# A two-layer graph network: the own half normalised in a later stage, counts and ranks from summed one-hots, and a new order of the sorting stage

## The chip, the cores and the metric

The kernel runs on one core of a Trainium2 chip. TensorE (PE) multiplies matrices and loads its weights (PEld), VectorE (DVE), ScalarE (ACT) and GpSimd (POOL) work elementwise, and SyncE (SP) issues most transfers. The metric is the device time of one execution in microseconds, the median of several. Lower is better.

## The reference

There are 12500 nodes with 256 features and 200000 edges `src`, `dst`, sorted by `dst`. The first layer, cut to what matters (4 heads of 32):

```python
feat = relu(einsum('nd,ohdk->ohnk', feat_in, W) + b)        # o = 0: own half, o = 1: neighbour half
att_s = leaky(feat[0] . a_self); att_n = leaky(feat[1] . a_neigh)
edge_w = (att_s[:, row] + att_n[:, col]) * adj_vals          # row = src, col = dst
agg = segment_sum(edge_w * feat[1][:, col], row)
feat = stack([feat[0], agg])
feat = (feat - mean) * scale * rsqrt(var + 1e-9) + offset    # per head, both halves
x = layernorm(x + concat(own half, aggregated half))
```

The second layer:

```python
messages = relu(concat(x[src], x[dst]) @ W_msg + b_msg)
h = relu(concat(x, segment_sum(messages, dst)) @ W_upd + b_upd)
x = layernorm(x + layernorm(h) * gamma + beta)
```

## The kernel before

The work runs in three stages, one after the other.

**Sorting stage.** The edges are sorted by `dst` but the first layer sums by `src`, so this stage writes every message into a log in DRAM, placed by the block of 128 source nodes that it belongs to (98 blocks). It goes over 112 groups of 14 tiles of 128 edges. `sort_tasks(g)` makes, for a group, the one-hots `A` of the blocks of its edges (`widen`, `hot`, `hot_b`: partition = edge, 14 tiles x 99 blocks, the first seven tiles in one instruction and the last seven in another). `ranks` counts the edges of each block with 14 matmuls of a 99-column one-hot with a column of ones. `quarter` and `rows` make log rows of the counts. `begins` adds, for each block, 14 matmuls of a triangular matrix with the one-hots. `place_mm0` to `place_mm2` and 14 `pick` instructions on ACT turn that into a slot for each edge, and `split`, `hot_r`, `hot_q`, `goods` and `permute` bring the edges' data into slot order. What is then needed as a row instead of a column, the destination of each slot, goes through DRAM and back: `rel_keep`, `rel_turn`, `rel_row`, `rel_out` (to `reld`), `rel_in` (back into `rr`, 512 KB, broadcast over the partitions), `hot_n` (one-hots `oT` of the destinations). Six `message` steps multiply these with the neighbour features (`F3`), six `evict` steps on ACT copy the result into the tile `m` (three buffers, of which `extras` on DVE writes two columns), and four `scatter` steps on POOL write `m` into the log.

Beside it, `feat_tasks(g)` computes the features: a window of destination nodes for the neighbour half, for all groups, and block `g` of nodes for the own half, for the first 98 groups. `transposes`, `keep`, `project`, `relu`, the attention sums and `centre` work on both halves at once. For the own half the stage also does the whole head normalisation and writes the first layer's partial result, `y` = x + offset + the normalised own half, to `yd` (`offsets`, `square`, `var`, `root`, `rstd`, `norm`, `scale`, `put`, `out_y`). `meta_tasks` prepares, once for eight groups, the edges' indices and weights (lines 325 to 406).

PE, ACT, DVE and SP run their instructions in the order in which the program gives them, written out by hand: the table `AT` gives each step a time in units of which a group has 256 (`TG`), all steps of all groups are sorted by `256 * g + AT[step]`, and each engine gets its instructions in this order. A step may stand several groups later than its group's first one. POOL's order is left to the framework.

**Middle stage.** It sums the log, block by block: five pieces to a block, loaded up to nine pieces ahead into twelve buffers (`log_load`), multiplied with attention on POOL (the fifth piece on DVE) and turned into one-hots on DVE (`log_hot`), and summed on PE two steps later (`log_sum`). Batches of up to four blocks then have their aggregated half normalised (`heads_a` to `heads_d`, the last on POOL), are added to `y`, which `load_y` fetches from `yd` with one load into three buffers, get the layernorm's sums, are multiplied with the message weights and stored (`proj_*`, `store_x1`). This order too is by steps: `work[t]` holds what is issued at step `t`, five steps to a block.

**Edge stage.** It gathers the projected source rows by edge, adds the destination part, applies relu, sums by destination and finishes the nodes.

Of the kernel before, what the change touches and what calls it, by code (L numbers as in the profile page):

```python
# [11 lines left out]
def _warn_once_fixed(msg, *args, **kwargs):  # L12
# [6 lines left out]
FT = mybir.dt.float32  # L19
FR = mybir.dt.float32r  # L20
BF = mybir.dt.bfloat16
I32 = mybir.dt.int32
AF = mybir.ActivationFunctionType
OP = mybir.AluOpType
AX = mybir.AxisListType

P = 128
D = 256
HD = 128
H = 4  # L30
GT = 14
# [6 lines left out]


AT = {  # L40
    "widen": -140, "hot": -47, "hot_b": 3, "ranks": 44, "quarter": 71, "rows": 78, "begins": 155,
    "keep_begins": 189, "keep_v": 180, "shift": 218, "reach": 377, "steps": 314, "steps_keep": 337,
    "steps_low": 358, "target": 474, "index": 554, "place_mm0": 207, "place_mm1": 281, "place_mm2": 370,
    "pick0": 224, "pick1": 255, "pick2": 256, "pick3": 299, "pick4": 305, "pick5": 305, "pick6": 312,
    "pick7": 368, "pick8": 401, "pick9": 408, "pick10": 435, "pick11": 456, "pick12": 457, "pick13": 481,
    "split": 523, "hot_r": 547, "goods": 577, "hot_q": 563, "permute": 636, "rel_keep": 663, "extras": 717,
    "rel_turn": 685, "rel_row": 708, "rel_out": 738, "rel_in": 884, "hot_n": 885, "message0": 965,
    "evict0": 985, "message1": 1004, "evict1": 1046, "message2": 1006, "evict2": 1074, "message3": 1051,
    "evict3": 1132, "message4": 1092, "evict4": 1150, "message5": 1140, "evict5": 1200, "scatter0": 1078,
    "scatter1": 1124, "scatter2": 1163, "scatter3": 1210, "load": -363, "transposes": 234, "keep": 250,  # L50
    "project": 290, "relu": 308, "offsets": 441, "att_mult": 334, "mean_sum": 371, "att_sum": 404,
    "centre": 388, "leaky_n": 494, "part0": 507, "part1": 678, "part2": 741, "part3": 780, "leaky_s": 899,
    "square": 476, "var": 595, "root": 656, "rstd": 792, "norm": 814, "scale": 916, "put": 941, "out_y": 1139,
    "m_load": -1372, "m_cast0": -982, "m_cast1": -1209, "m_col0": -970, "m_keep0": -940, "m_col1": -414,
    "m_keep1": -359, "m_col2": -655, "m_keep2": -607, "m_block": -852, "m_place": -776, "m_high": -348,
    "m_rest": -26, "m_mid": 2, "m_low": 358, "m_win": -179, "m_turn": -654, "m_pairs": -648, "m_mask": -313,
    "m_count": 101,
}
BIG = 4096.0
MAGIC = 1.5 * 2.0 ** 23  # L60
# [1 line left out]
BB = 4  # L62
# [40 lines left out]
def kernel(  # L103
# [19 lines left out]
    nc = tc.nc  # L123
    N = x.shape[0]
# [5 lines left out]
    ROWS = NB * P  # L130
# [10 lines left out]
    dram = ctx.enter_context(tc.tile_pool(name="dram", bufs=1, space=bass.MemoryType.DRAM))  # L141
    NBX = NB + 1
# [3 lines left out]
    reld = dram.tile([NG, P * NR], BF, name="reld")  # L146
    x1d = dram.tile([ROWS, D], FT, name="x1d")
    pd = dram.tile([ROWS, D], FT, name="pd")
    yd = dram.tile([ROWS, D], FT, name="yd")

    def bcast_row(ap1d, n):
        return ap1d.rearrange("(o n) -> o n", o=1).to_broadcast([P, n])
# [17 lines left out]
    epsh = consts.tile([P, 1], FT, name="epsh")  # L170
# [23 lines left out]
    scb = consts.tile([P, D], FT, name="scb")  # L194
    ofb = consts.tile([P, D], FT, name="ofb")
# [22 lines left out]
    with ExitStack() as l0:  # L218
# [3 lines left out]
        feat = l0.enter_context(tc.tile_pool(name="feat", bufs=2))  # L222
        srt = l0.enter_context(tc.tile_pool(name="srt", bufs=2))
# [14 lines left out]
        lessb = dcp.tile([P, P], BF, name="lessb")  # L238
        onesb = dcp.tile([P, 1], BF, name="onesb")
# [174 lines left out]
        xb = {}  # L414
        F3 = {}
# [13 lines left out]
        def feat_tasks(g):  # L429
# [4 lines left out]
            st = {}  # L434
# [20 lines left out]
                nc.scalar.copy(xT[:, a:z].rearrange("p c q -> p (c q)"), st["tp"][:, a * P:z * P])  # L455
                st["xT"] = xT

            def offsets():
                st["y"] = feat.tile([P, D], FT, name="y", bufs=3)
                nc.vector.tensor_tensor(st["y"], xb[g], ofb, op=OP.add)  # L460

            def project():
                fp = bank[g][:, 0:D] if ww else ps.tile([P, 512], FT, name="fs")[:, 0:D]
                nc.tensor.matmul(fp[:, lo:hi], ones3, bias3[:, lo:hi], start=True, stop=False)
# [52 lines left out]
                a = st["a"][:, 0:H]  # L517
                nc.vector.scalar_tensor_tensor(atts[:, g, :], a, 0.2, a, op0=OP.mult, op1=OP.max)

            def square():  # L520
                st["q"] = feat.tile([P, HD], FT, name="q")
                nc.scalar.activation(st["q"], st["F"][:, 0:HD], AF.Square)

            def var():
                st["v"] = feat.tile([P, H], FT, name="v")
                nc.vector.tensor_reduce(st["v"], st["q"].rearrange("p (h k) -> p h k", h=H), AX.X, OP.add)

            def root():
                nc.scalar.activation(st["v"], st["v"], AF.Sqrt, bias=epsh, scale=1.0 / 32)

            def rstd():
                nc.vector.reciprocal(st["v"], st["v"])

            def norm():
                c = st["F"][:, 0:HD].rearrange("p (h k) -> p h k", h=H)
                nc.vector.tensor_tensor(c, c, st["v"][:, :, None].to_broadcast([P, H, 32]), op=OP.mult)

            def scale():
                c = st["F"][:, 0:HD]
                nc.vector.tensor_tensor(c, c, scb[:, 0:HD], op=OP.mult)  # L540

            def put():
                nc.vector.tensor_tensor(st["y"][:, 0:HD], st["y"][:, 0:HD], st["F"][:, 0:HD], op=OP.add)

            def out_y():
                nc.sync.dma_start(yd[g * P:(g + 1) * P, :], st["y"])

            w = lambda f: f if ww else None
            k = lambda f: f if bb else None
            return dict(transposes=transposes, keep=keep, project=project, relu=relu, offsets=k(offsets),  # L550
                        att_mult=att_mult, mean_sum=mean_sum, att_sum=att_sum, centre=centre, leaky_n=w(leaky_n),
                        part0=w(part(0)), part1=w(part(1)), part2=w(part(2)), part3=w(part(3)),
                        leaky_s=k(leaky_s), square=k(square), var=k(var), root=k(root), rstd=k(rstd),
                        norm=k(norm), scale=k(scale), put=k(put), out_y=k(out_y))

        scatters, zeros = [], []
        zero = dcp.tile([P, RW * MW], FT, name="zero")
# [10 lines left out]
        def sort_tasks(g):  # L568


            c, j = divmod(g, GC)
            tl = slice(j * GT, (j + 1) * GT)
            st = {}
# [6 lines left out]
            h = GT // 2  # L580
# [9 lines left out]
            def hot_b():  # L590
                b = blk[c][:, j * GT + h:j * GT + GT, None].to_broadcast([P, h, NBX])
                nc.vector.tensor_tensor(st["A"][:, h:], iotab[:, h:], b, op=OP.is_equal)  # L592
                st["C"] = [st["A"][:, i] for i in range(GT)]

            def ranks():
                bank[g] = ps.tile([P, 512], FT, name="fs")
                st["sm"] = bank[g][:, D + P:]
                st["V"] = bank[g][:, D:D + NBE]
                for i, v in enumerate(st["C"]):
                    nc.tensor.matmul(st["sm"][:NBX, 0:1], v, onesb, start=(i == 0), stop=(i == GT - 1))  # L600

            def quarter():
                nc.scalar.activation(small("rows"), st["sm"][:NBX, 0:1], AF.Identity, bias=quart[:NBX], scale=1.0 / RW)
# [5 lines left out]
            def begins():  # L609
                r = st["rows"]  # L610
                nc.tensor.matmul(st["sm"][:NBX, 1:2], less[:NBX, :NBX], r, start=True, stop=True)
                nc.tensor.matmul(st["V"], r.to_broadcast([NBX, P]), less4[:NBX, :NBE],
                                 start=True, stop=False)
                for i, v in enumerate(st["C"]):
                    nc.tensor.matmul(st["V"][:, :NBX], lessb, v, start=False, stop=(i == GT - 1))

            def keep_begins():
                st["b0"] = begun[:, g:g + 1]
# [126 lines left out]
            def scatter(k):  # L745
                def f():
# [7 lines left out]
                    for p in zeros[-16:] if g >= GZ else zeros[:nz0] if g < 2 else []:  # L754
                        tc.add_manual_dep(ins, p.name, sync_dep, reason="the rows left over are zero")
                return f

            tasks = dict(widen=widen, hot=hot, hot_b=hot_b, ranks=ranks, quarter=quarter,
                         rows=rows, begins=begins, keep_begins=keep_begins, keep_v=keep_v, shift=shift, reach=reach,
                         steps=steps, steps_keep=steps_keep, steps_low=steps_low, target=target, index=index)  # L760
            tasks.update((f"place_mm{i}", place_mm(i)) for i in range(3))
# [2 lines left out]
                         extras=extras, rel_turn=rel_turn, rel_row=rel_row, rel_out=rel_out, rel_in=rel_in, hot_n=hot_n)  # L764
# [33 lines left out]
        work = defaultdict(list)  # L798
# [113 lines left out]
    with ExitStack() as bar:  # L912
        lgp = bar.enter_context(tc.tile_pool(name="lgp", bufs=12))
        bw = bar.enter_context(tc.tile_pool(name="bw", bufs=2))
# [17 lines left out]
        NK = len(PART)  # L932
# [132 lines left out]
            nc.scalar.activation(t, ys[q][:, i], AF.Identity, bias=nmr[:, b:b + 1], scale=rsd[:, b:b + 1])  # L1065
            nc.sync.dma_start(x1d[b * P:(b + 1) * P, :], t)

        ys = {}

        def load_y(q):  # L1070
            b, n = spans[q]
            ys[q] = bw.tile([P, BB, D], FT, name="y", bufs=3)
            nc.sync.dma_start(ys[q][:, :n], yd[b * P:(b + n) * P, :].rearrange("(b p) w -> p b w", p=P))

        def centre_proj():

# [18 lines left out]
        for q, (b, n) in enumerate(spans):  # L1095
            t0 = (b + n) * NK + 3
            for d, f in ((0, heads_a), (1, heads_s), (2, heads_b), (3, heads_r), (4, heads_c), (5, heads_d),
                         (8, stats), (9, root), (10, rstd), (10, offset)):
                work[t0 + d].append(lambda q=q, f=f: f(q))
            work[b * NK].append(lambda q=q: load_y(q))  # L1100
            for i in range(n):
                for d, f in ((8, proj_t), (9, proj_k), (11, proj_m), (13, proj_s), (13, store_x1)):
                    work[t0 + d + (NK - 1) * i].append(lambda b=b, i=i, f=f: f(b + i))
            tend = max(tend, t0 + 13 + (NK - 1) * (n - 1))
# [512 lines left out]
```

## Time and profile before

| | |
|---|---|
| median of 3 runs | 4087.51 us (4082.6 to 4089.36) |
| profiled execution | 4089.95 us, span 4088.2 us |
| granted TensorE clock, mean | 0.989 |
| busy over the span | PE 88%, DVE 78%, POOL 62%, ACT 60% |
| first sum of the middle stage | 1155.4 us |
| last sum of the middle stage | 2062.1 us |

The profile page gives busy times by engine, the span in slices, the chain of waits that ended last and the costliest groups of instructions. A group is named by its line, engine and operation, with the tile written, an arrow and the tiles read. The shares over the whole span mix three stages with different limits, so what a change is worth has to be read from the busy times and waits of its own stage.

### The profile page before, as it was taken

To read this page: it belongs to the slowest core of one execution; us is meant where nothing else is said; L and a number is where in the kernel's file an instruction comes from. 1 tells how busy PE (TensorE), PEld (TensorE's weight loads), DVE (VectorE), ACT (ScalarE), POOL (GpSimd) and SP (SyncE) were. 2 spreads that over 40 slices of the span, in tenths; PEclk is the share of its full clock that TensorE was granted. 3 is DMA by queue.
4 is the path that set the end of the run, shared out by engine and by line. 5 is a ranking of instruction groups with operands and counts; after the bars stand their busy time and mean duration, and the time that the engine had idled before them with its cause. 6 is when DMAs were issued, how large, how long until landed. Compare 5 with 4: busy or idle time off the path is not lost.

```text
span 4088.2 us, 86328 instructions
## 1 busy us (share of the span) xinstructions
PE 3580.6 (88%) x26432; PEld 3016.1 (74%) x26432; DVE 3197.3 (78%) x9815; ACT 2465.8 (60%) x8632; POOL 2549.4 (62%) x2461
## 2 busy tenths in 40 slices
PE   7999999999989999999978878787888787787776
PEld 6888888887878888888866666666666666666665
DVE  8999999999878888888856666667666666666666
ACT  7999999999922222222246555555565555555555
POOL 2555555554455555555557777777777777777775
PEclk9999999999999999999999999999999999999999
DMA  5777766665566666666656666666666666666664
GB/s 183 261 259 260 258 221 209 208 209 192 195 204 183 186 185 180 184 186 185 182 148 169 171 171 171 169 171 171 171 170 172 169 173 168 169 173 169 169 171 129
DMA packets 457248, 763.85 MB, mean 187 GB/s; under 512 B 75772, under 2 KB 300574, under 8 KB 456782
## 3 DMA queue, kind: packets, MB, share of 16 engines
q1 hardware_dynamic: 326622, 415.17, 35.7%
q0 software_dynamic: 110848, 327.87, 26.2%
q10 hardware_dynamic: 19312, 15.21, 1.2%
q8 instruction: 216, 3.54, 0.4%
q14 instruction: 250, 2.05, 0.2%
HBM read 553.43 MB, written 204.54 MB: 185 GB/s over the span
## 4 chain that ended last, share of the span: by engine, by line
PE 34%; DMA 24%; DVE 23%; ACT 8%; issue 5%; POOL 4%; DVEq 0%; ACTq 0%; POOLq 0%; SPq 0%
DMA gb<-pd,srcf 21%; PE sum L966 20%; PE agg L1364 6%; DVE gb L1345 4%; POOL gb L1286 4%; ACT gb L1347 3%; DVE mv L685 2%; PE qp L1323 2%; PE qm L1054 2%; ACT junk L667 2%; DVE qh L690 2%; DMA rr<-reld 1%; DVE oT L725 1%; DVE A L592 1%; DMA reld<-rT 1%
## 5 line engine op out<-in xcount | busy, mean ns | idle before, releaser
L1286 POOL DMA_INDIRECT gb<-pd,srcf x1563 | 1510.2, 966 | 511.5 <-issue 266.8
L1364 PE MATMUL agg<-gb,o 128*128 128x256 f32 x3126 | 860.6, 398 | 271.5 <-ACT gb L1347 268.4
L1345 DVE TENSOR_TENSOR gb<-qp,gb 128x512 f32<-128x512 f32 x781 | 538.5, 690 | 653.6 <-DMA gb<-pd,srcf 501.0
L1347 ACT ACTIVATE gb<-gb 128x512 f32<-128x512 f32 x781 | 491.1, 629 | 797.6 <-DVE gb L1345 795.7
L747 POOL DMA_INDIRECT log<-m,ix x448 | 563.6, 1258 | 582.4 <-ACT m L741 386.9
L1364 PEld LDWEIGHTS agg<-gb,o 128*128 128x128 f32 x3126 | 556.0, 191 | 493.2 <-ACT gb L1347 433.3
L966 PE MATMUL sum<-lg,o 128*128 128x256 f32 x3724 | 836.8, 378 | 11.5 <-DVE o L958 11.5
L966 PEld LDWEIGHTS sum<-lg,o 128*128 128x128 f32 x3724 | 696.3, 189 | 109.3 <-POOL lg L953 11.7
L958 DVE TENSOR_SCALAR o<-iotap,lg 128x128 f32<-128x128 f32 x1862 | 627.9, 402 | 123.8 <-PE sum L966 113.8
L953 POOL TENSOR_TENSOR lg<-lg 128x512 f32<-128x512 f32 x392 | 410.3, 1059 | 418.7 <-DMA lg<-log 238.2
L1323 PE MATMUL qp<-qh,oT 128*128 128x256 f32 x1563 | 544.0, 370 | 2.1 <-DVE oT L1310 2.1
L667 ACT ACTIVATE junk<-wp,nbig 128x99 bf16<-128x99 f32 x1568 | 543.5, 352 | 1.9 <-PE wp L640 1.8
L734 PE MATMUL mp<-F,oT 128*128 128x132 bf16 x5376 | 406.4, 221 | 17.5 <-DVE oT L725 13.7
L1323 PE MATMUL qp<-ql,oT 128*128 128x256 f32 x1563 | 406.7, 283 | 0.0
L734 PEld LDWEIGHTS <-oT 128*128 128x128 bf16 x5376 | 349.6, 99 | 47.9 <-DVE oT L725 16.4
L667 ACT ACTIVATION_READ_ACCUMULATOR junk<-wp,nbig 128x1 f32 x1568 | 328.7, 210 | 0.0
L741 ACT COPY m<-mp 128x396 f32<-128x396 f32 (+1 forms) x672 | 313.7, 467 | 14.3 <-PE mp L734 13.9
L1323 PEld LDWEIGHTS qp<-qh,oT 128*128 128x128 f32 x1563 | 299.4, 192 | 20.3 <-DVE oT L1310 2.5
L1323 PEld LDWEIGHTS qp<-ql,oT 128*128 128x128 f32 x1563 | 299.5, 192 | 17.9
L1310 DVE TENSOR_SCALAR oT<-dr,baseP 128x256 fp32r<-128x256 int32 x782 | 288.7, 369 | 10.6 <-DMA dr<-in_dst_dram 10.6
L1331 ACT ACTIVATE o<-iotac,rel 128x128 f32<-128x128 f32 x782 | 266.0, 387 | 1.9 <-issue 1.5
L973 ACT COPY S<-sum 128x256 f32<-128x256 f32 x98 | 36.5, 373 | 337.6 <-PE sum L966 337.6
(253 smaller groups left out, 6429.5 us busy)
## 6 DMA issues: line engine op xcount, KB each, us to landing
lg<-log SPq DMA_DIRECT2D x392, 268.0 KB
dr<-in_dst_dram SPq DMA_DIRECT2D x781, 128.0 KB
rr<-reld SPq DMA_DIRECT2D x112, 512.0 KB
log<-zero SPq DMA_DIRECT2D x101, 268.0 KB
gb<-pd,srcf POOLq DMA_INDIRECT x1563
lg<-log SPq DMA_DIRECT2D x98, 201.0 KB
xw<-in_x_dram SPq DMA_DIRECT2D x112, 128.0 KB
xw<-x1d SPq DMA_DIRECT2D x112, 128.0 KB
```

The source lines that it names most:

```text
L667: nc.scalar.activation(small("junk", NBX, BF, p=P), st["w", i][:, k * NBE:k * NBE + NBX], AF.Relu, bias=nbig, accum_out=st["sl"][:, t:t + 1])
L734: nc.tensor.matmul(mp[:, r * (HD + H):(r + 1) * (HD + H)], st["oT"][:, r0 + r], F3[g][:, k], start=(k == 0), stop=(k == 2))
L741: nc.scalar.copy(st["m"][:, r0:r0 + n, 0:HD + H], st.pop(("mp", i))[:, :n * (HD + H)].rearrange("p (r w) -> p r w", r=n))
L747: ins = nc.gpsimd.indirect_dma_start(out=log[:, :], out_offset=bass.IndirectOffsetOnAxis(ap=st["ix"][:, k:k + 1], axis=0), in_=st["m"][:, ...
L953: e.tensor_tensor(t[:, 1, :n, 0:HD].rearrange("p r (h k) -> p r h k", h=H), t[:, 0, :n, 0:HD].rearrange("p r (h k) -> p r h k", h=H), t[:, ...
L958: nc.vector.tensor_scalar(o[:, r], iotap, t[:, 0, r, MW - 2:MW - 1], t[:, 0, r, MW - 1:MW], op0=OP.is_equal, op1=OP.mult)
L966: nc.tensor.matmul(sums[b], o[:, r], t[:, :, r, 0:HD], start=(k == 0 and r == 0), stop=(k == NK - 1 and r == n - 1))
L1286: nc.gpsimd.indirect_dma_start(out=gb[s][:r, i], out_offset=None, in_=pd[:, :], in_offset=bass.IndirectOffsetOnAxis(ap=srci[:r, t:t + 1], ...
L1323: nc.tensor.matmul(qp[:r, i], oT[:, i * P:i * P + r], q, start=(k == 0), stop=(k == 1))
L1345: nc.vector.tensor_tensor(z, qp, z, op=OP.add)
L1347: nc.scalar.activation(z, z, AF.Relu)
L1364: nc.tensor.matmul(agg[g], o[:r, i], z[:r, i], start=(j == 0 and i == 0), stop=lastmm)
```

## The change

- In the sorting stage the own half is only centred. `out_f` stores this centred half, 128 columns, to a new DRAM tensor `selfd`. `offsets`, `square`, `var`, `root`, `rstd`, `norm`, `scale`, `put` and `out_y` are gone, and so is `yd`.
- In the middle stage `load_y` loads the nodes' rows straight from the input `x` and the centred half from `selfd`, four steps earlier than before and with four buffers for `y`. `own_s` to `own_d` normalise it in the batches that the stage already has: squares and roots on ACT, sums, reciprocals and the product on DVE, offsets, scale and the final addition on POOL.
- A new step `pair` on DVE adds the first seven one-hots of a group to the last seven. `ranks` and `begins` run over the seven sums instead of the 14 one-hots.
- Nearly every entry of the table `AT` is new.

```diff
-    "begins": 155, "keep_begins": 189, ... "rel_row": 708, "rel_out": 738, "rel_in": 884, "hot_n": 885,
-    "extras": 717, ... "message0": 965, ... "evict5": 1200, ... "scatter3": 1210, "load": -363, "transposes": 234,
+    "begins": 27, "keep_begins": 85, ... "rel_row": 603, "rel_out": 637, "rel_in": 801, "hot_n": 856,
+    "extras": 566, ... "message0": 927, ... "evict5": 1234, ... "scatter3": 1242, "load": -101, "transposes": 107,
...
-            def offsets(): ... square, var, root, rstd, norm, scale, put
-            def out_y():
-                nc.sync.dma_start(yd[g * P:(g + 1) * P, :], st["y"])
+            def out_f():
+                nc.sync.dma_start(selfd[g * P:(g + 1) * P, :], st["F"][:, 0:HD])
...
-                st["C"] = [st["A"][:, i] for i in range(GT)]
+            def pair():
+                st["B"] = srt.tile([P, h, NBX], BF, name="B")
+                nc.vector.tensor_tensor(st["B"], st["A"][:, :h], st["A"][:, h:], op=OP.add)
+                st["C"] = [st["B"][:, i] for i in range(h)]
...
-                    nc.tensor.matmul(st["sm"][:NBX, 0:1], v, onesb, start=(i == 0), stop=(i == GT - 1))
+                    nc.tensor.matmul(st["sm"][:NBX, 0:1], v, onesb, start=(i == 0), stop=(i == h - 1))
...
-                    nc.tensor.matmul(st["V"][:, :NBX], lessb, v, start=False, stop=(i == GT - 1))
+                    nc.tensor.matmul(st["V"][:, :NBX], lessb, v, start=False, stop=(i == h - 1))
...
-            ys[q] = bw.tile([P, BB, D], FT, name="y", bufs=3)
-            nc.sync.dma_start(ys[q][:, :n], yd[b * P:(b + n) * P, :].rearrange("(b p) w -> p b w", p=P))
+            y = ys[q] = bw.tile([P, BB, D], FT, name="y", bufs=4)
+            fs[q] = bw.tile([P, BB, HD], FT, name="fs")
...
+                nc.sync.dma_start(y[:, :m], x[b * P:(b + m) * P, :].rearrange("(b p) w -> p b w", p=P))
+            nc.sync.dma_start(fs[q][:, :n], selfd[b * P:(b + n) * P, :].rearrange("(b p) w -> p b w", p=P))
+        def own_s(q):
...
+            nc.scalar.activation(own[q][0][:, :n], fs[q][:, :n], AF.Square)
+        def own_b(q):
...
+            nc.vector.tensor_reduce(v[:, :n * H].rearrange("p (b h) -> p b h", h=H),
+                                    t[:, :n].rearrange("p b (h k) -> p b h k", h=H), AX.X, OP.add)
+        def own_r(q):
...
+            nc.scalar.activation(v[:, :n * H], v[:, :n * H], AF.Sqrt, bias=epsh, scale=1.0 / 32)
+        def own_c(q):
...
+            nc.vector.reciprocal(v[:, :n * H], v[:, :n * H])
+            nc.vector.tensor_tensor(F3, F3, v[:, :n * H, None].to_broadcast([P, n * H, 32]), op=OP.mult)
+        def own_o(q):
...
+            nc.gpsimd.tensor_tensor(y, y, ofb[:, None, :].to_broadcast([P, n, D]), op=OP.add)
+        def own_d(q):
...
+            nc.gpsimd.tensor_tensor(F, F, scb[:, None, 0:HD].to_broadcast([P, n, HD]), op=OP.mult)
+            nc.gpsimd.tensor_tensor(y, y, F, op=OP.add)
...
-            work[b * NK].append(lambda q=q: load_y(q))
+            t1 = b * NK
+            for d, f in ((-4, load_y), (2, own_s), (3, own_b), (4, own_r), (5, own_c), (1 + n // 2, own_o),
+                         (6 + 2 * (n > 1), own_d)):
+                work[t1 + d].append(lambda q=q, f=f: f(q))
```

## The prediction

> **What bounds the kernel now.** I read the busy time by stretch first. Sorting runs to about 1147 us, the middle stage to about 2062, the edge stage to the end.
>
> ```profile
> 600.00:1000.00 400.00, 385.60 (x5029) 333.99 (x5026) 393.84 (x1351) 391.98 (x1926) 202.40 (x162) 1.00 0.61 206
> 1600.00:2000.00 400.00, 400.00 (x1897) 348.31 (x1896) 345.84 (x1028) 88.44 (x205) 210.47 (x195) 1.00 0.64 184
> ```
>
> Columns: stretch, length, busy PE, PEld, DVE, ACT, POOL, clock, DMA share, GB/s. In sorting DVE (98.5%), ACT (98.0%) and PE (96.4%) are all full: cutting one alone would give little. In the middle PE is busy 400 of 400 us, ACT 22%, POOL 53%. The edge stage is not touched.
>
> Next, the DVE timeline of sorting, for the period of a group (start, duration, operation):
>
> ```profile
> 514.52 1.09 DVE L690 TENSOR_TENSOR qh<-iotaq,q 128x1792 bf16<-128x1792 bf16 x1
> 523.66 1.11 DVE L690 TENSOR_TENSOR qh<-iotaq,q 128x1792 bf16<-128x1792 bf16 x1
> 594.08 1.08 DVE L690 TENSOR_TENSOR qh<-iotaq,q 128x1792 bf16<-128x1792 bf16 x1
> ```
>
> Eight groups, one turn of the metadata, take 594.08 - 514.52 = 79.56 us: 9.95 us a group. A group without metadata takes 9.14 (the first two lines), with no gap on DVE. The metadata instructions of lines 325 to 406 sum to 7.0 us per eight groups in the DVE groups, about 5.6 without the 0.08 us by which neighbours overlap, so 0.70 a group. DVE's load is 9.84 of 9.95: it sets the pace. ACT's is 98% of 9.95 = 9.75, right behind.
>
> **The change part by part.** Durations overlap, so I cost an instruction by the step to its neighbour's start.
>
> ```profile
> 510.10 0.28 DVE L540 TENSOR_TENSOR F<-F,scb 128x128 f32<-128x128 f32 x1
> 510.30 0.40 DVE L488 TENSOR_REDUCE a<-tm 128x8 f32<-128x256 f32 x1
> ...
> 511.03 0.41 DVE L460 TENSOR_TENSOR y<-xb,ofb 128x256 f32<-128x256 f32 x1
> 511.37 0.17 DVE L713 COPY m<-mp 128x16 f32<-128x16 f32 x1
> 511.57 0.50 DVE L588 TENSOR_TENSOR A<-iotab,bx 128x693 bf16<-128x693 bf16 x1
> 511.99 0.20 DVE L625 SCALAR_TENSOR_TENSOR dl<-pos,capc,begun 99x1 f32<-99x1 f32 x1
> ```
>
> *Own half out of sorting, groups 0 to 97.* DVE loses `scale`, `put` and `norm` (0.20 each, as L540), `offsets` (0.34), `var` (0.19) and `rstd` (0.09): 1.22 us a group. ACT loses `square` (511.09 to 511.31) and `root` (517.81 to 518.00): 0.41. The store on SP stays one issue, of 64 KB for 128; no engine waits for it.
>
> *One-hots summed, all 112 groups.* PE loses 7 of 14 matmuls in `ranks` and 7 of 14 in `begins`:
>
> ```profile
> 514.87 0.78 PE L600 MATMUL fs<-onesb,A 128*99 128x1 bf16 x14
> 515.63 0.33 PE L645 MATMUL fs<-dl,step 99*99 99x1 f32 x2
> ...
> 518.24 0.82 PE L615 MATMUL fs<-A,lessb 128*128 128x99 bf16 x14
> 518.99 0.22 PE L706 MATMUL tp<-identb,rs 128*16 128x128 bf16 x1
> ```
>
> Half of 0.76 and half of 0.75 is 0.76 us. DVE gains `pair`, 128x693 bf16 from two halves of one tile. The nearest rows are L588 (0.42, steps 511.57 to 511.99) and L592, mean 885 ns, slot 0.79, which writes the same second half but also reads a broadcast. `pair` reads plain data, as L588 does: I take 0.42 and keep 0.79. The second half starts 693 x 2 = 1386 bytes in, not a multiple of four. The Trainium skill's "VectorE: DVE Perf Modes", section "Mode 2×_1P", asks for 4-byte alignment for two results a cycle, which speaks for 0.79; its "Vector Engine (DVE) Microarchitecture Reference", section 5.1, reports that alignment makes no difference, which gives 0.42. By the first the total below would be that of the second rival, by the second it stands; no row of before settles it.
>
> *Loads after.* DVE 9.84 - 1.22 + 0.42 = 9.04; ACT 9.75 - 0.41 = 9.34; PE at most 0.964 x 9.95 = 9.59 - 0.76 = 8.83. ACT becomes the bound, with DVE 0.30 behind on average and above it in the metadata-heavy groups (their period is now 10.73, so DVE about 9.93). For those peaks I add 0.11, what the period now exceeds DVE's load by: 9.45. Saved: 9.95 - 9.45 = 0.50 a group; ends 0.41 (stalls stay) and 0.61 (none). Groups 0 to 97 give 97 periods: **-49 us** (-40 to -59). Groups 98 to 111 have no own half; ACT is full there (68.99 of 70 us in 1060 to 1130), so halved matmuls and `pair` fall beside it: 0.
>
> *Order.* `AT` changes nearly everywhere; in 256ths of a period, two gaps matter. From `rel_row` through the two transfers of destinations to `hot_n`: 177 before, 253 after, so 6.9 us becomes 9.3. The transfers need some 2.7 + 5.3 us in the chain of waits, plus a few SP issues: the write's landing and the queue (x loads, zero rows and `out_f` now ahead of `rel_in`, 0.4 us each) hide each other. This is the stall that goes:
>
> ```profile
> DVE oT L725 <- DMA rr<-reld: 15.4, 7, 5.3
> ```
>
> The waits of 1000 to 1150: 15.4 us in seven waits, the longest 5.3, at 1008, where PE and ACT stand too. The others are in ACT's shade; I count that one, **-4** (0 to -5). Next late there is ACT itself. The other gap shrinks: from `evict5` to `extras` three groups on, which reuses the message tile and so waits on DVE for the scatters: 285 before, 100 after, 3.7 us at the new period. Last scatters in 200 to 1000 end 1.6 us (median, 3.2 longest) after the evict's end by POOL's timeline, and land about 1.75 later in the chain: 3.4 of 3.45. Behind the waiting `extras` queue `pair`, `index` and `hot_n`, for which PE, then ACT's evicts, wait. A late scatter stalls DVE by up to 1.6, less its 0.30 of slack: **+4** (0 to +29, 0.3 a group). The drain after the last permute has a longer order: **+2** (0 to +5).
>
> *Own half into the middle.* Per batch of four blocks, 37.1 us of PE:
>
> ```profile
> L953 POOL TENSOR_TENSOR lg<-lg 128x512 f32<-128x512 f32 x216 | 226.0, 1058 | 236.0 <-DMA lg<-log 136.1 <-PE sum L966 79.0 <-DVE o L958 17.2
> L1014 POOL TENSOR_TENSOR A<-A,scb 128x512 f32<-128x512 f32 x14 | 21.9, 1563 | 0.0
> L1016 POOL TENSOR_TENSOR y<-y,A 128x512 f32<-128x512 f32 x14 | 17.7, 1267 | 1.1
> ```
>
> POOL (count, busy us, mean ns, idle before): `own_d` 1.56 + 1.27, `own_o`, twice the width, 2.5 to 3.1: 5.9 us, 16%, so 53% becomes 69%. DVE: `own_b` 0.68, `own_c` 0.24 + 0.69 (rows L994, L1007, L1008): 4.3%, 86.5% becomes 91%. ACT: 0.63 + 0.31. SP: one load of y becomes two, 256 KB more per batch, 4% of what DMA moves, and four steps earlier into four buffers. All lies under PE, if PE stays fed. POOL idles waiting for loads or for PE to free a tile (136.1 and 79.0 above): it runs several pieces ahead. `own_d` waits on POOL for DVE's `own_c`, with the products of later pieces behind it; PE reaches those last. POOL's longest run without a product, 2.8 + 2.8 us with `heads_d`, is three pieces of PE's 1.86 us each, and products take 1.06. The cover holds: **+1** (0 to +10); if it were gone, 25 batches x 5.9 = 148.
>
> *Sum.* -49 - 4 + 4 + 2 + 1 = -46 on the profiled execution's 4089.95 us (span 4088.2) is 4044; the median stands 2.4 lower: **4042**.
>
> **Rivals.** *The scatters take the place (slower).* `extras` waits on late scatters in most groups. For: the gap is cut to a third, and POOL's scatters take 0.96 to 3.8 us. Against: the median scatter just fits. Each 0.1 us of mean stall beyond 0.30 costs 9.7; at 0.8 the gain is gone; at 1.2 it is 0.9 x 97 = +87, less 46: 4087.5 + 41 = 4129. It decides from 0.8 us a group.
>
> *`pair` runs at half rate.* DVE 9.41, level with ACT, so stalls stay as now: 0.42 a group, -41, -38 in all: 4050.
>
> *The middle stage does not hide the work.* PE starves behind POOL. Against: the idle above. Half of the 148 us exposed gives 4042 + 74 = 4116.
>
> *The new order gives back what the work saves:* 4080 to 4095. For: the old one left 1 to 2% idle on three engines, which is hard to better.
>
> **How the numbers follow.** About 0.2% (8 us) is what a measurement can tell from no change. Forecast 0.60, half-rate `pair` 0.14 (faster too), scatters 0.14 and middle 0.05 (slower), order 0.07 (same). Faster 0.74, same 0.07, slower 0.19. The forecast's own range, from the ends above, is 4026 to 4070. For 8 in 10 I go to 4018 below (ends together, and a cleaner drain) and 4090 above, which leaves out the slower cases.
>
> **What would show it.** The L690 row (new line 663) every 9.3 to 9.5 us instead of 9.95; ACT above 98% and DVE near 95% busy in sorting; `pair` at about 0.51 us, 0.87 if at half rate; the first sum of the middle near 1110 us, not 1155; PE full in the middle, which keeps its 907 us; POOL there near 69%. I am wrong if DVE waits at `extras` (new line 686) for more than 0.8 us a group, if PE idles behind POOL's products, or if periods stay above 9.8.

## The result and the profile after

The changed kernel takes **4113.72 us** (median of 4 runs, 4112.78 to 4123.5) against 4088.44 us (4082.6 to 4092.74) for the kernel before: ratio 1.0072, 95% interval 1.0059 to 1.0085. It is 25 us slower, where 46 us faster had been forecast. The profiled execution took 4112.78 us with a span of 4111.0.

The loss is in the sorting stage. The first sum of the middle stage moves from 1155.44 to 1178.87 us (+23.4), the middle stage grows from 906.61 to 911.27 us (+4.7), and the edge stage, which nothing touched, is 5 us shorter in this execution (it varies between 2020 and 2026 us over all profiles below).

Busy time by stretch after the change; the columns are stretch, length, busy PE, PEld, DVE, ACT, POOL, clock, DMA share, GB/s:

```profile
200.00:600.00 400.00, 352.89 (x4249) 300.22 (x4247) 348.00 (x1088) 366.93 (x1762) 238.39 (x156) 0.97 0.71 237
600.00:1000.00 400.00, 364.81 (x4540) 310.78 (x4538) 370.62 (x1164) 387.38 (x1876) 258.61 (x165) 1.00 0.62 204
1600.00:2000.00 400.00, 400.00 (x1896) 348.34 (x1896) 381.53 (x1059) 95.88 (x223) 270.81 (x227) 1.00 0.66 191
```

In sorting nobody is full any more: DVE is 87 to 93% busy, where it was 98.5%, ACT 92 to 97%, PE 88 to 91%. The work did go, but waiting took its place. POOL alone is busier, 259 us in 600 to 1000 instead of 202, though it has the same scatters to issue.

The granted clock of PE is lower too while the waits are longest: 0.94 in 0 to 200 us and 0.97 in 200 to 600, where the kernel before has 1.00 and 0.99; in 600 to 1000 it is 1.00 in both.

DVE's timeline gives the period (start, duration, operation; line 663 is the old line 690):

```profile
215.38 1.09 DVE L663 TENSOR_TENSOR qh<-iotaq,q 128x1792 bf16<-128x1792 bf16 x1
1014.38 1.08 DVE L663 TENSOR_TENSOR qh<-iotaq,q 128x1792 bf16<-128x1792 bf16 x1
```

Between these lie 79 groups: 10.11 us a group. From the 20th to the 100th group the mean is 9.98 us before and 10.09 after; by the 20th group the new kernel is already 9.9 us behind. So 9.9 + 8.9 (80 x 0.11) + 3.3 (the last twelve groups) + 1.3 (the drain) make the 23.4.

What DVE waited for in 200 to 1000 us (us in total, times, longest):

```profile
DVE m L686 <- DMA log<-m,ix: 42.0, 37, 3.2
DVE m L686 <- ACT junk L640: 8.4, 6, 2.1
DVE m L686 <- ACT F L502: 7.3, 6, 1.7
DVE m L686 <- ACT m L714: 4.4, 6, 1.3
```

Line 686 is `extras`, the first instruction that writes a message tile `m` anew, and `log<-m,ix` are the scatters that still read that tile. The kernel before has no wait there; all that its DVE waits for in 200 to 1000 is

```profile
DVE oT L725 <- DMA rr<-reld: 4.5, 9, 1.4
```

In the changed kernel DVE waits at `extras` for 62.6 us in some 79 groups, **0.79 us a group**. I read the three ACT rows as the same wait: `extras` needs nothing of those ACT instructions, they are only what the records name last. The long waits for `rr` in 1000 to 1150 us, 15.4 us in seven before, are down to one of 4.4.

One such wait in full. POOL's timeline, then DVE's, then the chain of waits (in brackets the idle time before, and its releaser):

```profile
471.38 1.01 POOL L720 DMA_INDIRECT log<-m,ix  x1 [0.30 <-ACT junk L640]
474.02 2.70 POOL L720 DMA_INDIRECT log<-m,ix  x1 [1.62 <-ACT m L714]
```

```profile
473.56 1.32 DVE L658 TENSOR_TENSOR mv<-rh,em 128x1120 bf16<-128x1120 bf16 x1
474.79 1.09 DVE L663 TENSOR_TENSOR qh<-iotaq,q 128x1792 bf16<-128x1792 bf16 x1
475.79 0.42 DVE L483 TENSOR_REDUCE a<-tm 128x8 f32<-128x256 f32 x1
...
480.45 0.19 DVE L686 COPY m<-mp 128x16 f32<-128x16 f32 x1 [1.07 <-DMA log<-m,ix]
...
480.66 0.52 DVE L565 TENSOR_TENSOR B<-A 128x693 bf16<-128x693 bf16 x1
481.09 0.15 DVE L633 TENSOR_TENSOR ix<-fs,roww 128x4 int32<-128x4 f32 x1
```

```profile
474.02 6.32 DMA log<-m,ix
```

The last scatter of a tile is released by the last evict at 474.02, just as DVE works on `mv` and `qh`. It takes 2.70 us instead of 0.96 and ends at 476.72, which is 0.93 us after `qh` gives way to the next instruction: as if it had begun only then. Its data land at 480.34, 3.6 us later, and `extras`, which had stood since 479.4, starts.

In 200 to 1000 us the scatters' mean goes from 1.28 to 1.56 us on POOL's timeline, and those above 1.9 us from 34 of 322 to 95 of 320. Of the 92 that overlap `mv`, 90 take more than 1.2 us. The last scatters of a tile show it best: of 80 in 200 to 1000 us none overlapped `mv` before and 68 do after, and their median goes from 1.21 to 2.50 us.

### The profile page after: what moved, and what is told of

It reads as the page before. It is cut to its first block, busy times and chain, and to the rows that moved or that the text cites. A ratio compares the mean times of both kernels' runs of the same rounds, so it can differ in the third digit from the quotient of the medians.

```text
span 4111.0 us, 82606 instructions
## 1 busy us (share of the span) xinstructions
PE 3541.8 (86%) x24864; PEld 2960.1 (72%) x24864; DVE 3215.7 (78%) x9421; ACT 2461.8 (60%) x8490; POOL 2787.2 (68%) x2542
## 3 DMA queue, kind: packets, MB, share of 16 engines
q8 instruction: 203, 3.33, 0.4%
## 4 chain that ended last, share of the span: by engine, by line
PE 35%; DMA 27%; DVE 13%; ACT 12%; issue 7%; POOL 6%; DVEq 0%; SPq 0%; POOLq 0%; ACTq 0%
DMA gb<-pd,srcf 20%; PE sum L939 19%; PE agg L1385 6%; DMA log<-m,ix 5%; POOL gb L1307 4%; DVE gb L1366 4%; ACT junk L640 4%; ACT gb L1368 3%; PE qp L1344 2%; PE qm L1027 2%; POOL log L720 2%; DVE mv L658 1%; ACT m L714 1%; DVE qh L663 1%; PE mp L670 1%
## 5 line engine op out<-in xcount | busy, mean ns | idle before, releaser
L720 POOL DMA_INDIRECT log<-m,ix x448 | 670.8, 1497 | 497.8 <-ACT m L714 274.8
L931 DVE TENSOR_SCALAR o<-iotap,lg 128x128 f32<-128x128 f32 x1862 | 613.6, 401 | 45.2 <-PE sum L939 36.9
L926 POOL TENSOR_TENSOR lg<-lg 128x512 f32<-128x512 f32 x392 | 428.1, 1105 | 232.0 <-DMA lg<-log 157.0
L640 ACT ACTIVATE junk<-wp,nbig 128x99 bf16<-128x99 f32 x1568 | 565.0, 385 | 2.1 <-PE wp L613 1.9
L640 ACT ACTIVATION_READ_ACCUMULATOR junk<-wp,nbig 128x1 f32 x1568 | 377.6, 243 | 0.0
```

What stands on the lines that cost most here:

```text
L640: nc.scalar.activation(small("junk", NBX, BF, p=P), st["w", i][:, k * NBE:k * NBE + NBX], AF.Relu, bias=nbig, accum_out=st["sl"][:, t:t + 1])
L720: ins = nc.gpsimd.indirect_dma_start(out=log[:, :], out_offset=bass.IndirectOffsetOnAxis(ap=st["ix"][:, k:k + 1], axis=0), in_=st["m"][:, ...
L926: e.tensor_tensor(t[:, 1, :n, 0:HD].rearrange("p r (h k) -> p r h k", h=H), t[:, 0, :n, 0:HD].rearrange("p r (h k) -> p r h k", h=H), t[:, ...
L931: nc.vector.tensor_scalar(o[:, r], iotap, t[:, 0, r, MW - 2:MW - 1], t[:, 0, r, MW - 1:MW], op0=OP.is_equal, op1=OP.mult)
```

## The experiments

All times are medians, each compared with runs of the kernel before on the same chip.

### What the moved work alone is worth: the old order

*The whole new work in the order of before* (`pair` put at 24, `out_f` in `out_y`'s place at 1139):

```diff
-    "widen": -233, "hot": -204, "hot_b": -204, "pair": -174, ... (the new AT)
+    "widen": -140, "hot": -47, "hot_b": 3, "pair": 24, ... "out_f": 1139, ... (the AT of before)
```

> All of the changed work (own half in the middle stage, seven summed one-hots), but with the table of times of the kernel before; pair stands at 24, between hot_b and ranks, out_f where out_y stood. Theory A and rival B: the gap from evict5 to extras is 285 again, so sorting gains what the prediction counted, 0.4 to 0.55 us a group: 4040 to 4055 us. Rival C: 4088 us or more.

Measured: 4037.78 us, 2 us below the range for theory A and rival B, ratio 0.9871 (0.9854 to 0.9887), first sum at 1106.0. Its period from the 20th to the 100th group is 9.45 us. Stretch 600 to 1000:

```profile
600.00:1000.00 400.00, 377.15 (x4663) 321.63 (x4663) 382.24 (x1215) 391.74 (x1944) 218.40 (x170) 0.99 0.61 208
```

The work is worth 50 us. ACT, DVE and PE stand in the forecast's order: 9.34, 9.04 and 8.83 us in a period of 9.45 would be 395, 383 and 374 of 400, and 392, 382 and 377 are measured. The new order therefore costs 76 us over the old one, work for work.

*Only the own half moved* (the 14 one-hots and the old order kept, the middle stage as in the changed kernel):

```diff
-    "square": 476, "var": 595, ... "put": 941, "out_y": 1139,
+    "out_f": 1139,
...
-                nc.sync.dma_start(yd[g * P:(g + 1) * P, :], st["y"])
+                nc.sync.dma_start(selfd[g * P:(g + 1) * P, :], st["F"][:, 0:HD])
```

> The kernel before with only the own half moved into the middle stage (14 one-hots, old table of times). DVE 8.62 and ACT 9.34 us a group, PE as before at up to 9.59: theory A and rival B expect PE or ACT to bind, 9.5 to 9.65 us a group, 4050 to 4065 us. Rival C (the middle stage pays): its length grows from 907 us by 20 or more and the time stays at 4088 or above.

Measured: 4036.42 us, ratio 0.9868 (0.9852 to 0.9885), first sum at 1101.2. That is the same as with `pair`, and 14 us less than expected. The expectation took PE's busy time before, 9.59 us a group, for work that stays; with the same matmuls it is now 392 of 400 us in 600 to 1000, 9.25 of a period of 9.43. With `pair` it is 377, 8.91 a group: `pair` takes 0.34 us off PE's busy time, not 0.76.

*Only `pair`* (everything else as before):

```diff
-                st["C"] = [st["A"][:, i] for i in range(GT)]
+            def pair():
+                st["B"] = srt.tile([P, h, NBX], BF, name="B")
+                nc.vector.tensor_tensor(st["B"], st["A"][:, :h], st["A"][:, h:], op=OP.add)
```

> The kernel before with only the one-hots summed (pair at 24). If DVE sets the pace of sorting, as the prediction's loads say (9.84 of 9.95 us), 0.42 us more on it cost 0.42 x 112 = 47 us: about 4135 us, and 0.79 a group or 4175 if pair runs at half rate. If PE sets it, 0.76 us less on PE make it faster, 4020 to 4060 us. If ACT does, no change, 4088.

Measured: 4129.65 us, ratio 1.0094 (1.0077 to 1.0111), 42 us slower. In 600 to 1000:

```profile
600.00:1000.00 400.00, 365.57 (x4292) 307.41 (x4290) 394.94 (x1332) 380.64 (x1854) 216.23 (x157) 0.96 0.59 201
```

DVE is still 98.7% busy and everyone else has gone slack. 112 x 0.42 = 47 us of DVE work cost 42 us: before the change DVE sets the pace, and relief for PE buys nothing.

### Where the new order loses its 76 us: tiles that scatters hold

*The changed kernel with a fourth `m`:*

```diff
-        msgp = l0.enter_context(tc.tile_pool(name="msgp", bufs=3))
+        msgp = l0.enter_context(tc.tile_pool(name="msgp", bufs=4))
```

> The changed kernel with four buffers for the message tile in place of three. Theory A (the new order writes a message tile again, with extras, too soon after its last scatter, and DVE stands there): the wait at extras, 0.8 us a group now, falls below 0.1, the period goes from 10.1 to about 9.5 us, the first sum of the middle stage from 1179 to 1120 to 1135 us, the time from 4114 to 4055 to 4070 us. Rival B (the new order as a whole is worse, the wait at extras only shows it and moves elsewhere): within 10 us of 4114. Rival C (the moved work itself costs the time): also within 10 us of 4114.

Measured: 4080.74 us, ratio 0.9979 (0.9969 to 0.9989), 33 us better than the changed kernel, but 43 short of the same work in the old order. That lies between what theory A (4055 to 4070) and the rivals (within 10 of 4114) expected. DVE's longest wait in 200 to 1000 us:

```profile
DVE ix L633 <- DMA log<-m,ix: 30.8, 28, 2.3
```

The wait at `extras` is gone, and the next instruction that scatters can hold is late: `index` writes `ix`, the rows that they read. That tile has four buffers; in the table `scatter3` and the `index` four groups later lie 123 units apart in the new order and 368 in the old one. I had not looked at this gap before the result.

*The changed kernel with six `ix`, `m` left at three:*

```diff
-                nc.vector.tensor_tensor(small("ix", RW, I32, bufs=4, p=P), st["sm"][:, 4:4 + RW], roww, op=OP.add)
+                nc.vector.tensor_tensor(small("ix", RW, I32, bufs=6, p=P), st["sm"][:, 4:4 + RW], roww, op=OP.add)
```

> The changed kernel with six ix and m left at three. If the m tile is the one that binds first: no gain, 4105 to 4120 us, with DVE's wait at the extras on the transfer as in the changed kernel. If ix is what binds and m only follows: 4070 to 4090.

Measured: 4121.0 us, ratio 1.0069 (1.0046 to 1.0092): nothing gained, as expected where `m` binds first (1 us above that range). `extras` comes ahead of `index` and binds first.

*Both:* four `m` and six `ix`.

> The changed kernel with four buffers for the message tile and six for the index tile ix. With four message tiles alone the wait moved from extras to index, which also waits for the scatters (38 us in 200 to 1000). Theory A (reuse of tiles that scatters read is all that is wrong with the new order): both waits gone, first sum of the middle stage near 1110 us, 4035 to 4050 us, level with the old order. Rival D (the new order has other faults too, such as scatters under two long DVE operations): still 4060 to 4080 us.

Measured: **4029.11 us**, ratio 0.9865 (0.9848 to 0.9881), first sum at 1089.4. The longest of what DVE still waits for in 200 to 1000 (the rest is 3.7 us, on ACT), and the stretch 600 to 1000:

```profile
DVE oT L698 <- DMA rr<-reld: 8.9, 14, 1.7
```

```profile
600.00:1000.00 400.00, 378.14 (x4765) 325.41 (x4766) 389.82 (x1242) 397.00 (x1985) 232.08 (x174) 1.00 0.64 213
```

Two numbers in the program give 85 us: ACT is 99% busy, as forecast, and the period is 9.28 us. This version beats both kernels.

*The control: the same buffers in the kernel before.*

> The kernel before, with four buffers for m and six for ix and nothing else. If buffers only matter because the new order shortened the reuse distance of m and ix: no change, 4080 to 4095 us, first sum of the middle near 1155 us as in the kernel before. If the buffers help any order (a rival to the new order as the cause): faster by 20 us or more.

Measured: 4086.83 us, ratio 1.0000 (0.999 to 1.0009). The old order has nothing to gain from buffers, so what they cure is the new order's doing.

### What makes the scatters late

*`mv` and `qh` 32 places earlier in the changed kernel*, so that they no longer lie where the last scatter is released:

```diff
-    "split": 374, "hot_r": 384, "goods": 423, "hot_q": 429, ...
+    "split": 374, "hot_r": 384, "goods": 391, "hot_q": 397, ...
```

> The changed kernel with goods and hot_q (mv and qh on DVE) 32 units earlier, at 391 and 397, so that they should be over when the last scatter of a group starts. Theory E (a scatter on POOL cannot proceed while certain DVE operations run, and the new order puts the last scatter under mv and qh): its mean falls from 1.56 us in 200 to 1000 to 1.2 to 1.35, the wait at extras from 62 us to below 35, the time from 4114 to 4080 to 4100 us. Rival F (the scatters are long for want of DMA or POOL time): mean within 0.1 of 1.56, time within 8 us of 4114.

Measured: 4097.68 us, ratio 1.0028 (1.0017 to 1.004), about 18 us better than the changed kernel. The scatters' mean falls from 1.56 to 1.20 us, with 9 of 324 above 1.9, but the wait at `extras` only from 63 to 44 us, where theory E expected less than 35. (Its profiled execution, at 4084.62 us, is its fastest.) One such wait in the chain:

```profile
416.26 5.67 DMA log<-m,ix
```

On POOL's timeline the scatter takes 1.04 us of that, so the landing 4.63. So duration is a part of the lateness, and the landing is another. Over all such pieces of the chain in 200 to 1000 us the medians are: before (4 pieces) scatter 1.4 and landing 2.0; after (34) 2.25 and 3.33; here (36) 1.08 and 3.91. These are the pieces that bind, so they are longer than the mean.

For the landing I have only a correlation. The transfers that SP issues come in one bunch, since SP stands at `rel_out` until the destinations are there; two rows of the changed kernel's SP timeline:

```profile
471.21 1.10 SPq L531 DMA_DIRECT2D log<-zero  x1
...
472.93 0.72 SPq L694 DMA_DIRECT2D rr<-reld  x1
```

With the two loads of x before them (256 KB) and the 64 KB of `selfd` between them, these are 1100 KB just ahead of the scatter at 474.02. Of the 34 pieces after, the half with the shorter landings (mean 2.5 us) has 215 KB of such issues in the 4 us up to the scatter's end, the half with the longer ones (4.0 us) 537 KB; with `mv` and `qh` earlier it is 449 KB for 3.0 us and 973 KB for 4.9. The zero rows are issued until 556 us, and after that the wait at `extras` is 23 us in 400 instead of 39. But the granted clock is also full only from then on (0.97 in 200 to 600, 1.00 in 600 to 1000), and with `pair` alone, where DVE never waits for a scatter and PE is idle for 34 to 39 of 400 us, it is 0.96 to 0.98, so a low clock comes without these waits too. No run took the bunch away by itself or held the clock, so how much of the landing, and of the longer waits in the first half, is due to either stays open.

*The same two steps earlier, with four `m` and six `ix`:*

> The changed kernel with four m, six ix, and mv and qh put 32 places of 256 earlier, so that the last scatter no longer lies beside them. If scatters cost time only through the tiles that they hold: within 10 us of the run with four m and six ix alone (4029), since nothing waits on them there any more. If a scatter that is shorter also frees POOL for the goods of the next group: 4010 to 4019.

Measured: 4028.98 us, ratio 0.9857 (0.984 to 0.9873), the same as with the buffers alone, though the scatters' mean is 1.20 instead of 1.37 us. Here a slow scatter costs time only through the tile that it holds.

*The scatter by itself*: a small kernel that computes nothing of the reference. It issues eight scatters of the kernel's shape beside a stream of one kind of DVE instruction, and repeats this for each kind:

```diff
+        nc.vector.tensor_tensor(o16[:, 0:1792], a16[:, 0:1792], b16[:, 0:1792], op=OP.add)      # and six others
...
+            ins = nc.gpsimd.indirect_dma_start(
+                out=log[:, :], out_offset=bass.IndirectOffsetOnAxis(ap=ix[:, k:k + 1], axis=0), in_=m, in_offset=None).ins
```

> A small kernel of its own that computes none of the reference: eight scatters of 128 rows of 2144 bytes on POOL, repeated while DVE runs back to back, in turn: nothing, bf16 additions of two tiles in SBUF, bf16 products of two broadcast tiles, bf16 comparisons with a column, fp32 additions of two tiles in SBUF, fp32 additions with one input in PSUM, fp32 reductions, and two-input scalar operations. Theory E expects 0.96 us for a scatter beside nothing, the PSUM input and the reduction, and a scatter drawn out by the DVE operation that runs (1 us or more longer) beside operations with two inputs in SBUF. Rival F expects 0.96 to 1.1 us beside each of them.

POOL's timeline: a scatter beside nothing, two beside `TENSOR_TENSOR` on 1792 bf16 with both inputs in SBUF (where the two durations alternate), one beside a `TENSOR_SCALAR` on 2048 bf16, and one beside `TENSOR_TENSOR` on 512 fp32 with one input in PSUM:

```profile
13.77 0.96 POOL L100 DMA_INDIRECT log<-m,ix  x1 [0.30 <-issue]
...
51.18 1.82 POOL L100 DMA_INDIRECT log<-m,ix  x1 [0.30 <-issue]
53.30 0.96 POOL L100 DMA_INDIRECT log<-m,ix  x1 [0.30 <-issue]
...
107.77 1.27 POOL L100 DMA_INDIRECT log<-m,ix  x1 [0.30 <-issue]
...
165.09 0.96 POOL L100 DMA_INDIRECT log<-m,ix  x1 [0.30 <-issue]
```

Beside the broadcast bf16 product of `mv`'s shape it is 1.73 us once and then 1.05; beside fp32 with both inputs in SBUF 1.15, in either form; beside a reduction 0.96. The most is 0.86 us more, less than a full microsecond and half of the 1.74 that the kernel shows under `mv` and `qh`: here a scatter waits for the rest of one instruction, there for two in a row. In DVE's records the instructions beside the scatter of 1.82 us start at 51.07 and 52.19, and the scatter ends at 52.99, 0.80 after the second start; beside the broadcast product (76.50 and 77.29), the `TENSOR_SCALAR` (108.17 and 109.04) and fp32 (133.60 and 134.40) it is 0.79 to 0.87. So the kinds that draw a scatter out differ by how long the instruction under way still had to run. Why it does not slip in between `mv` and `qh` stays open; in the run with both earlier, where a short fp32 instruction lies between them, the scatter shown above (416.26) does.

### Two smaller questions

*`hot_n` later in the old order.* The new work in the old order still waits 23.7 us for `rr` (200 to 1000):

```diff
-    "rel_in": 884, "hot_n": 885, "message0": 965,
+    "rel_in": 884, "hot_n": 915, "message0": 965,
```

> All of the changed work with the old table of times, but hot_n at 915 in place of 885, so that the transfers of destinations have 207 units in place of 177. In this kernel with 885, DVE waits 23.7 us for rr in 200 to 1000. If that wait is on the path: most of it goes and the time falls from 4038 to 4020 to 4032 us. If ACT (393 of 400 us busy) sets the pace anyhow: 4034 to 4042 us.

Measured: 4043.54 us, ratio 0.9899 (0.9882 to 0.9915), no better than without (0.9871), and 2 us above the range for ACT as the limit. The wait falls to 9.0 us, and the time does not follow: PE, then ACT's evicts, wait on `hot_n` instead.

*The best version without `pair`* (four `m`, six `ix`, the new order):

```diff
-            def pair():
-                st["B"] = srt.tile([P, h, NBX], BF, name="B")
-                nc.vector.tensor_tensor(st["B"], st["A"][:, :h], st["A"][:, h:], op=OP.add)
-                st["C"] = [st["B"][:, i] for i in range(h)]
+                st["C"] = [st["A"][:, i] for i in range(GT)]
```

> Four m and six ix in the new order, but with the one-hots and PE's rank as before (no pair sum). In the new order ACT sets the pace at 397 of 400 us and PE has 22 to spare; without the pair PE takes 0.76 us a group more (378 becomes about 409 of 400, so it would bind) and DVE loses 0.42. If PE then sets the pace: about 0.2 us a group slower, 4040 to 4055 us. If ACT still does: 4025 to 4035.

Measured: 4028.88 us, ratio 0.9856 (0.984 to 0.9873), the same as with it. In 600 to 1000:

```profile
600.00:1000.00 400.00, 395.87 (x5376) 350.81 (x5373) 375.15 (x1201) 396.99 (x1988) 240.01 (x175) 1.00 0.63 212
```

PE takes back what `pair` had saved, 396 of 400 us, and comes level with ACT without passing it. That PE would bind at 409 was wrong: the 14 matmuls more cost 18 us of PE's busy time in 400, 0.41 us a group, where 0.76 had been written.

## Why the prediction was wrong

**The step that failed is the scatter gap**, the "+4 (0 to +29)" from `evict5` to `extras`, in which "the median scatter just fits" with 3.4 of 3.45 us. It took two durations from a trace in which DVE did other work at that place. The last scatter ends 1.6 us after the evict in the old order (median); the new order puts it under `mv` and `qh`, where it takes 2.50 us instead of 1.21 and ends 2.8 us after the evict. And the 1.75 us for the landing was the shortest of the four pieces in the chain before, one of which has 3.5; in the new order it is 3.3 in the median of those that bind. In the example 2.7 and 3.6 us stand where 1.6 and 1.75 were written, 6.3 in a gap of 3.9 (100 of 256 units of the period). For the duration the cause is shown, by the two steps put earlier; for the landing it stays open.

The rows that could have told this were in the trace: it has scatters of 3.8 us, which the prediction names as an argument for the rival and then leaves out of the sum. Of the 29 above 2.2 us in 200 to 1000, 18 lie under both `mv` and `qh` and 10 under one of them; after the change there are 75, and 62 lie under both. The missing question was what DVE does at the moment at which the new order releases the scatter.

**A second step was not made at all.** `ix` is held by the scatters too, and its gap shrinks from 368 to 123 units. Of two tiles that the same transfers read, the prediction looked at one. The runs give 33 us for `m` alone, nothing for `ix` alone, 85 us for both: the two waits stand in a row, and removing the first exposes the second.

**The rival that came true** is "the scatters take the place". Its point of decision, 0.8 us of stall a group, is what was measured (0.79), and there it says that the gain is gone: by its own rule (0.79 - 0.30) x 97 = 48 us of loss against 46 of gain, hence no change. The measured loss is 73 us of sorting beyond the same work in the old order, 0.64 us a group from the 20th to the 100th (51 us) and 18 us by the 20th group. With both buffers the 20th group comes at 217.2 us, as in the old order (216.8), instead of 235.1, so these 18 us are the same waits. The slack of 0.30 which the rule grants does not show: from the 52nd to the 84th group, with the clock at 1.00, the changed kernel's period is 9.73 us and that of the version with both buffers 9.16, and the difference is the wait at `extras` there, 0.57 a group. DVE's stalls reach ACT in full; PE and then ACT's evicts stand behind `hot_n`.

**What held.** The order of the loads after the change; the 9.45 us a group (9.45 in the old order), hence the -49 (-50 in all measured with the new work in the old order); the end of most of the waits for `rr` in the new order; the drain (+1.3 for +2). Some of it is luck. The 9.45 is 9.25 of ACT and 0.20 of idle time where 9.34 and 0.11 were added. PE's 8.83 came out (8.91) because two errors offset each other: its busy time before, 9.59, fell to 9.25 with the own half alone, and `pair` took 0.34, not 0.76. And the 9.45 was meant for the new order, which with enough buffers runs at 9.28. That -4 for those waits would be gained is not shown: the order with enough buffers is 55 to 57 us below the kernel before, the old order 50 to 52, and the intervals overlap.

**`pair` runs at full rate.** 0.52 us in the record and 0.43 to the next start, as the plain row of before, though its second input begins 1386 bytes in. Of the two pages of the Trainium skill which the prediction set against each other, the "Vector Engine (DVE) Microarchitecture Reference" is borne out and the alignment rule of "VectorE: DVE Perf Modes" is not, for this instruction. PE's halved matmuls are seen too (0.78 and 0.82 for 14 before, lines 600 and 615):

```profile
502.52 0.45 PE L573 MATMUL fs<-onesb,B 128*99 128x1 bf16 x7
...
507.90 0.49 PE L588 MATMUL fs<-B,lessb 128*128 128x99 bf16 x7
```

The two rows are 0.66 us shorter, and 0.80 by the step to the next start, by which the 0.76 was costed. Yet PE's whole busy time falls by only 0.34 us a group in the old order and 0.41 in the new one; the rows of other matmuls get longer, and why is open. And the sum did not say that `pair` is worth nothing beside the own half's move, which the runs with and without it show in both orders: it takes from PE, which is not last once DVE is relieved, and gives to DVE, which is not last either.

**The middle stage** costs 3 to 5 us in every run that has the moved work, against +1 (0 to +10). PE stays full (400 of 400) and POOL is at 68%, as forecast (69%), but DVE is at 95% instead of 91%. The group of `own_o` on POOL and one product of DVE in 1200 to 2000 us, then the same product before (busy us, mean ns, idle before):

```profile
L1084 POOL TENSOR_TENSOR y<-y,ofb 128x1024 f32<-128x1024 f32 x22 | 52.0, 2362 | 41.5 <-DMA y<-in_x_dram 41.5
```

```profile
L926 DVE TENSOR_TENSOR lg<-lg 128x384 f32<-128x384 f32 x86 | 68.8, 800 | 0.0
```

```profile
L953 DVE TENSOR_TENSOR lg<-lg 128x384 f32<-128x384 f32 x87 | 56.0, 644 | 0.0
```

POOL's new instructions cost less than was written: 2.36 us for `own_o` (2.5 to 3.1), 1.26 and 1.27 for `own_d` (1.56 and 1.27). But the DVE product of line 926 takes 800 ns instead of 644, and that of line 981 takes 1432 instead of 686. The records show when: the 14 of line 926 beside which POOL does nothing take 550 ns in the mean, the 72 others 848; before, 33 take 551 and 54 take 701. The prediction priced the two engines as if they did not meet.

That is not where the 3 to 5 us go, though. By the copies of the sums on ACT, all but 0.1 us of the changed kernel's 4.7 arises in the first ten or so of the 98 blocks, some 100 us; from there to the last block the stage takes as long as before. In the first 110 us PE waits once before (first line), and after the change three times for DVE (second line) and twice for POOL, 2.0 us:

```profile
PE sum L966 <- DVE o L958: 11.5, 1, 11.5
```

```profile
PE sum L939 <- DVE o L931: 12.0, 3, 11.2
```

So PE's cover holds once the loads and products run ahead, as forecast, and fails a little while they do not yet. What delays DVE and POOL there was not tried.

## What to carry to other kernels

When an order is changed, list every tile that an asynchronous transfer reads, and for each compare the distance from that transfer to the next writer with the buffers that it has; then price the transfer by what the other engines will be doing at its new place, not by its mean at the old one. Before judging an order, give such tiles one or two buffers more: here the verdict on the order moved by 85 us with two numbers. And measure the moved work in the old order first, which separates what the work is worth from what the order costs.

## What the runs showed of the hardware

- An indirect scatter's issue on POOL, 0.96 us alone, is drawn out by DVE instructions beside it: to 1.82 us by bf16 `TENSOR_TENSOR` with both inputs in SBUF, to 1.27 by a bf16 `TENSOR_SCALAR`, to 1.15 by fp32 with both inputs in SBUF; not at all (0.96) by one with an input in PSUM or by a reduction. In the small kernel a scatter that is drawn out ends 0.79 to 0.87 us after the DVE instruction under way gives way; the last scatters of the changed kernel, 68 of 80 beside `mv`, take 2.50 us in the median. The Trainium skill's "SBUF — State Buffer", section "Who interferes with whom", says that a DVE instruction with two SBUF inputs contends with a GpSimd instruction that reads SBUF, and that reductions do not; these rows agree, and it is the rule that the prediction overlooked. The same section infers that descriptor generation is not held up by `tensor_tensor`; for this indirect scatter the measurement says otherwise.
- In the middle stage a DVE product with two SBUF inputs (line 926, 128x384 fp32) took 550 ns where POOL did nothing beside it and 848 where it did. With POOL at 68% instead of 53% its mean was 800 ns for 644, and that of line 981 1432 for 686.
